# Two cross-attention layers on one core: another order of work inside a step

## The chip, the cores and the metric

The kernel runs on one core of one Trainium2 chip. The metric is the device time of one execution in microseconds (us), and for several executions their median. The core has five engines with a queue each: TensorE (PE in the profile; PEld is its weight load), VectorE (DVE), ScalarE (ACT), GpSimd (POOL) and SyncE (SP, which here only starts transfers). A queue is worked in order: an instruction that has to wait holds up all that stands behind it on its engine.

## The reference, cut to what matters

All numbers are float32. There are 8 batches of 256 rows with 320 channels (20 heads of 16), and for each batch 256 context tokens of 512 numbers. Two layers follow each other.

```python
# layer 0: 77 text tokens, 179 image tokens, two softmaxes, one sum
q, k, v = x @ Wq.T, enc[:, :77] @ Wk.T, enc[:, :77] @ Wv.T
k_ip, v_ip = enc[:, 77:] @ Wk_ip.T, enc[:, 77:] @ Wv_ip.T
out = softmax(q k.T / 4) v + softmax(q k_ip.T / 4) v_ip      # per head
x1 = out @ Wo.T + bo + x
# layer 1: 252 text tokens, 4 image tokens
q, k, v = x1 @ W_q, enc[:, :252] @ W_k, enc[:, :252] @ W_v
p = softmax(q k.T / 4)                                        # per head
sem = l2norm(p @ enc[:, :252]) . l2norm(enc[:, 252:])
p_ip = softmax(q k_ip.T / 4 + 0.5 * sem) * spatial_mask
out = (p v + p_ip v_ip) @ W_out + b_out + x1
```

The norm in `sem` comes from a Gram matrix: |p E|^2 = sum over t of p_t (p G)_t, with G = E E^T. So each head of layer 1 has one product that gives p G, p v and the dot products with the image tokens at once.

## The kernel before, in words

**Units and steps.** A unit is four heads ("a quad") of one batch and one layer; there are five units per batch and layer, 40 per layer. The loop at the end of the kernel runs over steps n = 5b + s. Step n handles unit n of layer 0 and unit n - 6 of layer 1, and the second half of the layer-1 unit of the step before. From n = 40 on there is only layer 1 (`layer_1`), before that `both_layers` writes out a step.

**Order.** TensorE, VectorE, ScalarE and GpSimd keep the order in which the program issues (`manual_schedule`); only the transfers that SyncE starts are placed by the framework's scheduler. So the order of the calls in `both_layers`, and the table `plan` in `fillers`, are the order of each of the four queues.

**What a step does.** For a layer-0 unit: `l0_begin` multiplies queries and keys (16 products, L317) into the four PSUM tiles sc0 to sc3; `l0_max` takes row maxima on VectorE (8 reductions, L412); `l0_exp` takes exponentials on ScalarE, one pair of heads per call (8 instructions, L424); `l0_transposed` turns one pair's probabilities on TensorE (8 transposes into the same sc tiles, L355) and copies them out (L360: three of four on VectorE, one on ScalarE); `l0_values` multiplies with v (L442, tile oT) and ScalarE copies the result; in the next step `l0_attn` turns it back (L462, tile o), scales it on VectorE (L467) and adds the text and image parts on GpSimd (L477).
For a layer-1 unit: `scores1` begins it and takes the maxima of both pairs (L612, with a small copy, L615); `l1_exp` (L624, 4 instructions per pair); `l1_transposed`; and in the next step `l1_values(v1, j)` for each head j and each half of the rows: two TensorE products (L648, L651) into a tile y, which VectorE reads with a multiply-and-sum (L655) and a small copy (L659).

**Fillers.** Work of other stages of a batch (projections of k, v and q, the Gram matrix, output projections, the rest of layer 1's image attention) is put between these by `fillers(n, place)`: step s and place give a list of functions for the batch ahead, now, last or old (b + 1, b, b - 1, b - 2). Nearly all of them write a tile "mm" on TensorE, which VectorE or ScalarE then copies out.

**PSUM.** sc0 to sc3 have one buffer each, the tiles "mm" two, and y, oT and o together two (tag "y"):

```python
ps_sc = ctx.enter_context(tc.tile_pool(name="ps_sc", bufs=1, space=PS))
ps_mm = ctx.enter_context(tc.tile_pool(name="ps_mm", bufs=2, space=PS))
ps_y = ctx.enter_context(tc.tile_pool(name="ps_y", bufs=2, space=PS))
```

So a tile "mm" can be written once the one two before it has been copied out, and the same holds for the tiles "y". The transposed attention and x tiles (`attn_T`, `transposed`) use "mm" too, one tile per half of the rows.

**Transfers.** `load_batch(b)` reads the transposed x and the transposed context of batch b, on SyncE (for batch 1 on ScalarE). It is called in step s = 3 of the batch before (s = 2 for batch 1). xT has one buffer, which it shares with the transposed x1; encT has two.

Of the kernel before, what the change touches and what calls it, by code (L numbers as in the profile page):

```python
# [8 lines left out]
F32 = mybir.dt.float32  # L9
# [41 lines left out]
def kernel(  # L51
# [67 lines left out]
    def load_batch(b, eng):  # L119
        r = {}  # L120
        r["xT"] = io.tile([P, NC, S], F32, tag="xT", name=f"xT_{b}", bufs=1)
        eng.dma_start(
            out=r["xT"][:, 0:2, :], in_=xT[b, 0:256, :].rearrange("(m p) s -> p m s", p=P)
        )
        eng.dma_start(out=r["xT"][:, 2, :], in_=xT[b, CH[2] :, :])
        r["encT"] = io.tile([P, NE, T], F32, tag="encT", name=f"encT_{b}")
        eng.dma_start(out=r["encT"], in_=encT[b].rearrange("(k p) t -> p k t", p=P))
        return r
# [9 lines left out]
    bat = {0: load_batch(0, nc.sync)}  # L138
# [345 lines left out]
    def l0_attn_T(b):  # L484
        r = bat[b]
        r["aT"] = [attn_T(r["attn"][:, half, :], f"p0_{b}_{half}") for half in range(NH)]

    def l0_out(b):
        r = bat[b]
        r["x1"] = bp.tile([P, NH, C], F32, tag="x1", name=f"x1_{b}")  # L490
        for half in range(NH):
            project_out(
                r["aT"][half], wo, r["x"][:, half, :], r["x1"][:, half, :], f"p0_{b}_{half}"
            )
# [248 lines left out]
    def l1_attn_T(b):  # L743
        r = bat[b]
        r["aT1"] = [attn_T(r["attn1"][half], f"p1_{b}_{half}") for half in range(NH)]

    def l1_out(b, half):
        r = bat[b]
        osb = work.tile([P, C], F32, tag="attn1", name=f"osb_{b}_{half}", bufs=3)
        project_out(r["aT1"][half], wo1, r["x1"][:, half, :], osb, f"p1_{b}_{half}")  # L750
        nc.sync.dma_start(out=out[b, half * P : (half + 1) * P, :], in_=osb)
# [24 lines left out]
    def fillers(n, place):  # L776
# [4 lines left out]
            (0, 1): [(l0_q, now, (2,)), (l0_attn_T, last)],  # L781
            (0, 2): [(l0_out, last)],
            (0, 3): [(l1_k, last, 0)],
            (0, 4): [(l1_xT, last)],
            (0, 5): [(l1_q, last, (0, 1))],
            (1, 0): [(l0_k, now, 1)],
            (1, 1): [(l1_k, last, 2)],
            (1, 3): [(l1_k, last, 1)],
            (1, 4): [(l1_gram, now, 0)],
            (2, 0): [(l1_v, now, 0)],  # L790
            (2, 1): [(l1_q, last, (2,)), (l1_norm, old)],
            (2, 3): [(l0_k, now, 2)],
            (2, 4): [(l1_fused, old)],
            (3, 0): [(l0_v, ahead, 0)],
            (3, 1): [(l1_v, now, 1), (l1_probs, old)],
            (3, 2): [(l1_probs_T, old)],
            (3, 3): [(l0_q, ahead, (0, 1))],
            (3, 4): [(l1_attn, old), (l1_image, now)],
            (4, 0): [(l0_k, ahead, 0)],
            (4, 1): [(l1_gram, now, 1), (l1_attn_T, old)],  # L800
            (4, 2): [(l1_out, old, 0)],
            (4, 3): [(l0_v, ahead, 1)],
            (4, 4): [(l1_out, old, 1)],
        }
        if n < NQ - 1:
# [6 lines left out]
                (1, 3): [(image_tokens, 0)],  # L812
# [5 lines left out]
                (3, 3): [(l0_q, 1, (0, 1)), (l1_image, 0)],  # L818
# [19 lines left out]
    def scores1(n):  # L838
# [4 lines left out]
        home = 1 if n < N0 else n % 2  # L843
        u = l1_begin(*divmod(n - SHIFT, NQ), home)
        for pair in range(2):
            l1_max(u, pair)
        return u

    def both_layers(n, u, v1):
# [6 lines left out]
        part(l0_attn, u)  # L856
        part(l1_values, v1, 0)
        l0_exp(u0, 1)
        part(l1_values, v1, 1)
        l0_transposed(u0, 0)  # L860
        fillers(n, 1)
        part(l1_values, v1, 2, (0,))
        l0_transposed(u0, 1)
        part(l1_values, v1, 2, (1,))
        qz[1] = queries(1, n)
        qz[0] = queries(0, n + 1)
        fillers(n, 2)
        u1 = scores1(n)
        part(l1_exp, u1, 0)
        fillers(n, 3)  # L870
        part(l1_exp, u1, 1)
        part(l1_values, v1, 3, (0,))
        part(l1_transposed, u1, 0)
        fillers(n, 4)
        part(l1_values, v1, 3, (1,))
        part(l1_transposed, u1, 1)
        fillers(n, 5)
# [4 lines left out]

# [91 lines left out]
```

## Time and profile before

| | us |
|---|---|
| median of 3 runs (lowest, highest) | 961.18 (959.59, 962.16) |
| the profiled execution: its own time | 962.78 |
| its span, first to last instruction | 961.1 |
| PE busy | 912.3 |
| DVE busy | 632.3 |
| ACT busy | 533.2 |
| POOL busy | 199.3 |

The mean granted TensorE clock was 0.986. Busy time of PE includes time in which a product waits for its weights, so it isn't all work. The timeline lists instructions by start; "xN" merges N instructions of one line, and a bracket gives the idle time of that engine just before and what ended it. Records of one engine overlap a little, so a duration in a stream is best read as the distance from one start to the next. In full batches the steps s = 0 to 4 take 26.04, 20.63, 20.27, 22.11 and 22.69 us, read from one oT (L442) to the next: 111.74 us a batch.

### The profile page before, as it was taken

How to read it: one execution, taken by the hardware profiler on the slowest of the kernel's cores; microseconds unless marked ns; L12 is line 12 of the kernel's file. 1: busy time of each engine (PE TensorE's matmuls, PEld its weight loads, DVE VectorE, ACT ScalarE, POOL GpSimd, SP SyncE). 2: the span in 40 equal slices, each digit the busy share in tenths (PEclk: the TensorE clock that was granted, in tenths of full speed). 3: DMA queues.
4: the chain of work that ended last, by engine and by line, in shares of the span. 5: the costliest groups of instructions: out<-in, count | busy, mean ns of one | idle time of the engine just before them, and what ended most of it. 6: DMA issues, size and time to landing. Idle time of an engine off the chain costs nothing.

```text
span 961.1 us, 18793 instructions
## 1 busy us (share of the span) xinstructions
PE 912.3 (95%) x6296; PEld 722.4 (75%) x6296; DVE 632.3 (66%) x2127; ACT 533.2 (55%) x2314; POOL 199.3 (21%) x336
## 2 busy tenths in 40 slices
PE   7888999999999999999999999999999999889885
PEld 5566678788787877778787887878777887667773
DVE  2344467766776677767776668766777677764864
ACT  3476466656554675546755566546655467433540
POOL 5421221222111221122211221112211222102100
PEclk9799999999999999999999999999999999999997
DMA  7310010001000010000100010000100000000000
GB/s 263 97 45 1 16 39 1 1 15 40 5 9 21 4 42 1 15 15 23 22 1 14 15 41 5 9 21 16 29 1 15 19 1 1 1 14 1 1 15 14
DMA packets 16847, 21.88 MB, mean 23 GB/s; under 512 B 1632, under 2 KB 15904, under 8 KB 16752
## 3 DMA queue, kind: packets, MB, share of 16 engines
q1 hardware_dynamic: 12048, 12.49, 4.9%
q0 software_dynamic: 1296, 4.25, 1.4%
q10 hardware_dynamic: 3408, 3.95, 1.2%
q8 instruction: 51, 0.84, 0.4%
q14 instruction: 44, 0.36, 0.1%
HBM read 17.24 MB, written 2.62 MB: 21 GB/s over the span
## 4 chain that ended last, share of the span: by engine, by line
PE 84%; ACT 8%; DVE 4%; issue 2%; DMA 1%; POOL 1%; ACTq 0%; DVEq 0%; POOLq 0%
PE y L648 15%; PE sc L355 13%; PE sc L317 9%; PE v L279 9%; PE y L651 7%; PE k L267 7%; PE q L249 6%; PE p_o L292 6%; PE oT L442 4%; ACT e L424 3%; ACT e L624 3%; PE g L525 2%; DVE nmx L612 2%; PE p_aT_ps L285 1%; DVE nmx L412 1%
## 5 line engine op out<-in xcount | busy, mean ns | idle before, releaser
L424 ACT ACTIVATE e<-sc,nmx 128x77 f32<-128x77 f32 (+1 forms) x640 | 227.6, 413 | 58.9 <-DVE nmx L412 58.9
L648 PE MATMUL y<-gv,et 126*128 126x272 f32 x640 | 210.3, 410 | 10.1 <-DVE num L659 6.0
L655 DVE CUSTOM_DVE_ANT_0 e<-y,e 128x252 f32<-128x252 f32 x320 | 134.3, 420 | 105.6 <-PE y L651 104.5
L624 ACT ACTIVATE e<-sc,nmx 128x252 f32<-128x252 f32 x320 | 147.2, 484 | 101.7 <-DVE aip L615 101.6
L355 PE MATMUL sc<-ident,e 128*126 128x128 f32 (+1 forms) x1280 | 173.5, 275 | 14.0 <-ACT e L424 7.8
L412 DVE TENSOR_REDUCE nmx<-sc 128x2 f32<-128x154 f32 x320 | 109.7, 416 | 97.2 <-PE sc L317 97.2
L360 DVE COPY et<-sc 128x512 f32<-128x512 f32 (+1 forms) x228 | 151.9, 688 | 23.3 <-PE sc L355 20.0
L355 PEld LDWEIGHTS sc<-ident,e 128*126 128x126 f32 (+1 forms) x1280 | 145.1, 140 | 26.2 <-ACT e L424 12.6
L424 ACT ACTIVATION_READ_ACCUMULATOR e<-sc,nmx 128x1 f32 x640 | 160.7, 251 | 0.0
L651 PEld LDWEIGHTS y<-gv,et 126*128 126x128 f32 x640 | 121.7, 190 | 26.2
L651 PE MATMUL y<-gv,et 126*128 126x146 f32 x640 | 132.0, 288 | 0.0
L648 PEld LDWEIGHTS y<-gv,et 126*128 126x128 f32 x640 | 102.3, 190 | 30.1 <-issue 11.1
L612 DVE TENSOR_REDUCE nmx<-sc 128x2 f32<-128x504 f32 x160 | 106.8, 676 | 26.6 <-PE sc L317 26.6
L360 ACT COPY et<-sc 128x512 f32<-128x512 f32 (+1 forms) x92 | 53.2, 585 | 96.4 <-PE sc L355 96.4
L317 PE MATMUL sc<-k,sc_qz 32*128 32x256 f32 x1280 | 99.3, 404 | 2.6 <-POOL sc_qz L306 2.5
L477 POOL TENSOR_TENSOR attn<-o_sb 128x64 f32<-128x64 f32 x80 | 24.0, 321 | 364.0 <-DVE o_sb L467 358.1
L317 PEld LDWEIGHTS sc<-k,sc_qz 32*128 32x128 f32 x1280 | 62.6, 185 | 33.6 <-issue 23.2
L306 POOL TENSOR_SCALAR sc_qz<-q,quad_m 128x256 f32<-128x256 f32 x80 | 73.1, 925 | 4.2 <-ACT q L256 4.2
L267 PE MATMUL k<-encT,wk 128*128 128x77 f32 (+1 forms) x384 | 72.7, 332 | 0.0
L624 ACT ACTIVATION_READ_ACCUMULATOR e<-sc,nmx 128x1 f32 x320 | 70.1, 219 | 0.0
L267 PEld LDWEIGHTS k<-encT,wk 128*128 128x128 f32 x384 | 57.9, 190 | 15.4 <-issue 12.0
L538 POOL COPY gv<-gv 126x3402 f32<-126x3402 f32 (+1 forms) x16 | 33.2, 2078 | 121.4 <-PE sc L355 71.5
(129 smaller groups left out, 1059.1 us busy)
## 6 DMA issues: line engine op xcount, KB each, us to landing
encT<-in_encT_dram SPq DMA_DIRECT2D x7, 512.0 KB
x<-in_x_dram SPq DMA_DIRECT2D x8, 320.0 KB
out_dram<-osb SPq DMA_DIRECT2D x16, 160.0 KB
xT<-in_xT_dram SPq DMA_DIRECT2D x7, 256.0 KB
xT<-in_xT_dram SPq DMA_DIRECT2D x7, 128.0 KB
vip_rows<-vipA SPq DMA_DIRECT2D x32, 25.0 KB
wk<-in_WkT_dram ACTq DMA_DIRECT2D x1, 640.0 KB
wkip<-in_WkipT_dram ACTq DMA_DIRECT2D x1, 640.0 KB
```

Source lines behind the costliest of these rows:

```text
L267: nc.tensor.matmul(ps[:, t0:t1], columns(w, k, m), encT_b[:, k, t0:t1], start=(k == 0), stop=(k == NE - 1),)
L279: nc.tensor.matmul(ps, lhsT(k), w[:, k, :], start=(k == 0), stop=(k == NE - 1))
L317: nc.tensor.matmul(sc[j][:, half, :], qz[rows, half * P : (half + 1) * P], kT(j)[rows, m, :], start=True, stop=True,)
L355: nc.tensor.transpose(v[:, c, half, :], u["e"][x][:, j, half, t0 + c * tn : t0 + (c + 1) * tn], ident,)
L360: copies[j](u["et"][x][:tn, j].rearrange("p c n s -> p (c n s)"), ps)
L412: nc.vector.tensor_reduce(u["nmx"][x][:, j, :, a], u["sc"][2 * x + j][:, :, t0:t1], AX.X, ALU.max, negate=True,)
L424: nc.scalar.activation(u["e"][x][:, j, half, t0:t1], u["sc"][2 * x + j][:, half, t0:t1], AF.Exp, bias=u["nmx"][x][:, j, half, a : a + 1], ...
L612: nc.vector.tensor_reduce(u["nmx"][x][:, j, :], sc[:, :, t0 : t0 + TXT1], AX.X, ALU.max, negate=True)
L624: nc.scalar.activation(u["e"][x][:, j, half, t0 : t0 + TXT1], u["sc"][2 * x + j][:, half, t0 : t0 + TXT1], AF.Exp, bias=u["nmx"][x][:, j, ...
L648: nc.tensor.matmul(y, et[:, 1 - odd, half, :], gv[0][:, g, full], start=True, stop=False)
L651: nc.tensor.matmul(y[:, into], et[:, odd, half, :], gv[1][:, g, part], start=False, stop=True)
L655: nc.vector.tensor_tensor_reduce(e, y[:, g0 : g0 + TXT1], e, op0=ALU.mult, op1=ALU.add, scale=1.0, scalar=0.0, accum_out=r["n2"][:, half, ...
```

## The change

- `both_layers` is written in another order. `l0_attn` moves from ahead of the first layer-1 products to behind them and a filler; the first two heads' products, which stood in a row, are now parted by a filler, `l0_attn` and the first transposes; the third head's two halves, which stood on either side of the second transposes, now both follow them. There are seven filler places in place of six.
- `scores1` is split into `begin1` and `max_exp1`, which takes the maxima and the exponentials of one pair. In `both_layers` no filler stands between the two pairs' exponentials any more. In `layer_1` two filler places come ahead of the scores, and the second pair's maxima move behind the first head's products.
- `l0_attn_T`, `l1_attn_T` and `l0_out` take one half of the rows per call, and the table puts the halves at different places.
- The table of fillers is rewritten: the Gram matrix' second part goes from step 4 to step 3, the next batch's first v from step 3 to step 2, and the places are renumbered; the table for the first four steps likewise.
- `load_batch` is split; the context of batch b + 1 is loaded in step s = 2.

```diff
@@ -116,16 +116,16 @@
     def load_e(t, w, eng):
         eng.dma_start(out=t[:, :, 0:C], in_=w.rearrange("(k p) c -> p k c", p=P))
 
-    def load_batch(b, eng):
-        r = {}
-        r["xT"] = io.tile([P, NC, S], F32, tag="xT", name=f"xT_{b}", bufs=1)
-        eng.dma_start(
-            out=r["xT"][:, 0:2, :], in_=xT[b, 0:256, :].rearrange("(m p) s -> p m s", p=P)
-        )
-        eng.dma_start(out=r["xT"][:, 2, :], in_=xT[b, CH[2] :, :])
-        r["encT"] = io.tile([P, NE, T], F32, tag="encT", name=f"encT_{b}")
-        eng.dma_start(out=r["encT"], in_=encT[b].rearrange("(k p) t -> p k t", p=P))
-        return r
+    def load_xT(b, eng):
+        t = io.tile([P, NC, S], F32, tag="xT", name=f"xT_{b}", bufs=1)
+        eng.dma_start(out=t[:, 0:2, :], in_=xT[b, 0:256, :].rearrange("(m p) s -> p m s", p=P))
+        eng.dma_start(out=t[:, 2, :], in_=xT[b, CH[2] :, :])
+        bat[b]["xT"] = t
+
+    def load_encT(b, eng):
+        t = io.tile([P, NE, T], F32, tag="encT", name=f"encT_{b}")
+        eng.dma_start(out=t, in_=encT[b].rearrange("(k p) t -> p k t", p=P))
+        bat[b]["encT"] = t
 
     def load_resid(b):
 
@@ -135,7 +135,9 @@
         for half in range(NH):
             nc.gpsimd.tensor_tensor(r["x"][:, half, :], r["x"][:, half, :], bo_b, ALU.add)
 
-    bat = {0: load_batch(0, nc.sync)}
+    bat = [{} for _ in range(B)]
+    load_xT(0, nc.sync)
+    load_encT(0, nc.sync)
     wq, wq1 = new_c("wq", HP), new_c("wq1", HP)
     wo, wo1 = new_c("wo"), new_c("wo1")
     wk, wkip, wk1 = new_e("wk", again=HP), new_e("wkip", again=HP), new_e("wk1", again=HP)
@@ -481,17 +483,17 @@
                 ALU.add,
             )
 
-    def l0_attn_T(b):
-        r = bat[b]
-        r["aT"] = [attn_T(r["attn"][:, half, :], f"p0_{b}_{half}") for half in range(NH)]
-
-    def l0_out(b):
-        r = bat[b]
-        r["x1"] = bp.tile([P, NH, C], F32, tag="x1", name=f"x1_{b}")
-        for half in range(NH):
-            project_out(
-                r["aT"][half], wo, r["x"][:, half, :], r["x1"][:, half, :], f"p0_{b}_{half}"
-            )
+    def l0_attn_T(b, half):
+        r = bat[b]
+        r["aT", half] = attn_T(r["attn"][:, half, :], f"p0_{b}_{half}")
+
+    def l0_out(b, half):
+        r = bat[b]
+        if half == 0:
+            r["x1"] = bp.tile([P, NH, C], F32, tag="x1", name=f"x1_{b}")
+        project_out(
+            r["aT", half], wo, r["x"][:, half, :], r["x1"][:, half, :], f"p0_{b}_{half}"
+        )
 
 
     def l1_k(b, m):
@@ -740,14 +742,14 @@
             attn = r["attn1"][half]
             nc.vector.tensor_tensor(attn, attn, ps[:, :C], ALU.add)
 
-    def l1_attn_T(b):
-        r = bat[b]
-        r["aT1"] = [attn_T(r["attn1"][half], f"p1_{b}_{half}") for half in range(NH)]
+    def l1_attn_T(b, half):
+        r = bat[b]
+        r["aT1", half] = attn_T(r["attn1"][half], f"p1_{b}_{half}")
 
     def l1_out(b, half):
         r = bat[b]
         osb = work.tile([P, C], F32, tag="attn1", name=f"osb_{b}_{half}", bufs=3)
-        project_out(r["aT1"][half], wo1, r["x1"][:, half, :], osb, f"p1_{b}_{half}")
+        project_out(r["aT1", half], wo1, r["x1"][:, half, :], osb, f"p1_{b}_{half}")
         nc.sync.dma_start(out=out[b, half * P : (half + 1) * P, :], in_=osb)
 
     msk = const.tile([P, NH], F32, tag="msk", name="msk")
@@ -778,29 +780,31 @@
         ahead, now, last, old = b + 1, b, b - 1, b - 2
         plan = {
             (0, 0): [(l0_v, now, 2)],
-            (0, 1): [(l0_q, now, (2,)), (l0_attn_T, last)],
-            (0, 2): [(l0_out, last)],
-            (0, 3): [(l1_k, last, 0)],
-            (0, 4): [(l1_xT, last)],
-            (0, 5): [(l1_q, last, (0, 1))],
+            (0, 1): [(l0_q, now, (2,))],
+            (0, 2): [(l0_attn_T, last, 0)],
+            (0, 3): [(l0_attn_T, last, 1), (l0_out, last, 0), (l0_out, last, 1)],
+            (0, 4): [(l1_k, last, 0)],
+            (0, 5): [(l1_xT, last)],
+            (0, 6): [(l1_q, last, (0, 1))],
             (1, 0): [(l0_k, now, 1)],
             (1, 1): [(l1_k, last, 2)],
-            (1, 3): [(l1_k, last, 1)],
-            (1, 4): [(l1_gram, now, 0)],
+            (1, 4): [(l1_k, last, 1)],
+            (1, 5): [(l1_gram, now, 0)],
             (2, 0): [(l1_v, now, 0)],
             (2, 1): [(l1_q, last, (2,)), (l1_norm, old)],
-            (2, 3): [(l0_k, now, 2)],
-            (2, 4): [(l1_fused, old)],
-            (3, 0): [(l0_v, ahead, 0)],
-            (3, 1): [(l1_v, now, 1), (l1_probs, old)],
-            (3, 2): [(l1_probs_T, old)],
-            (3, 3): [(l0_q, ahead, (0, 1))],
-            (3, 4): [(l1_attn, old), (l1_image, now)],
+            (2, 4): [(l0_k, now, 2)],
+            (2, 5): [(l0_v, ahead, 0), (l1_fused, old)],
+            (3, 0): [(l1_v, now, 1)],
+            (3, 1): [(l1_gram, now, 1), (l1_probs, old)],
+            (3, 3): [(l1_probs_T, old)],
+            (3, 4): [(l0_q, ahead, (0, 1))],
+            (3, 5): [(l1_attn, old), (l1_image, now)],
             (4, 0): [(l0_k, ahead, 0)],
-            (4, 1): [(l1_gram, now, 1), (l1_attn_T, old)],
-            (4, 2): [(l1_out, old, 0)],
-            (4, 3): [(l0_v, ahead, 1)],
-            (4, 4): [(l1_out, old, 1)],
+            (4, 1): [(l1_attn_T, old, 0)],
+            (4, 2): [(l1_attn_T, old, 1)],
+            (4, 3): [(l1_out, old, 0)],
+            (4, 4): [(l0_v, ahead, 1)],
+            (4, 5): [(l1_out, old, 1)],
         }
         if n < NQ - 1:
             plan = {
@@ -809,13 +813,13 @@
                 (0, 2): [(l0_v, 0, 2)],
                 (1, 0): [(l0_k, 0, 1)],
                 (1, 1): [(l0_q, 0, (2,))],
-                (1, 3): [(image_tokens, 0)],
+                (1, 4): [(image_tokens, 0)],
                 (2, 0): [(l1_gram, 0, 0)],
                 (2, 1): [(l1_v, 0, 0)],
                 (2, 2): [(l0_k, 0, 2)],
                 (3, 0): [(l1_v, 0, 1)],
                 (3, 1): [(l0_v, 1, 0)],
-                (3, 3): [(l0_q, 1, (0, 1)), (l1_image, 0)],
+                (3, 4): [(l0_q, 1, (0, 1)), (l1_gram, 0, 1), (l1_image, 0)],
             }
         for f, at, *args in plan.get((s, place), ()):
             if 0 <= at < B:
@@ -835,16 +839,16 @@
         if u is not None:
             f(u, *args)
 
-    def scores1(n):
+    def begin1(n):
 
         if qz[1] is None:
             return None
 
-        home = 1 if n < N0 else n % 2
-        u = l1_begin(*divmod(n - SHIFT, NQ), home)
-        for pair in range(2):
-            l1_max(u, pair)
-        return u
+        return l1_begin(*divmod(n - SHIFT, NQ), 1 if n < N0 else n % 2)
+
+    def max_exp1(u, x):
+        l1_max(u, x)
+        l1_exp(u, x)
 
     def both_layers(n, u, v1):
 
@@ -853,49 +857,50 @@
             l0_max(u0, pair)
         l0_exp(u0, 0)
         fillers(n, 0)
-        part(l0_attn, u)
         part(l1_values, v1, 0)
         l0_exp(u0, 1)
+        fillers(n, 1)
+        part(l0_attn, u)
+        l0_transposed(u0, 0)
         part(l1_values, v1, 1)
-        l0_transposed(u0, 0)
-        fillers(n, 1)
-        part(l1_values, v1, 2, (0,))
+        fillers(n, 2)
         l0_transposed(u0, 1)
-        part(l1_values, v1, 2, (1,))
+        part(l1_values, v1, 2)
         qz[1] = queries(1, n)
         qz[0] = queries(0, n + 1)
-        fillers(n, 2)
-        u1 = scores1(n)
-        part(l1_exp, u1, 0)
         fillers(n, 3)
-        part(l1_exp, u1, 1)
+        u1 = begin1(n)
+        part(max_exp1, u1, 0)
+        part(max_exp1, u1, 1)
+        fillers(n, 4)
         part(l1_values, v1, 3, (0,))
         part(l1_transposed, u1, 0)
-        fillers(n, 4)
+        fillers(n, 5)
         part(l1_values, v1, 3, (1,))
         part(l1_transposed, u1, 1)
-        fillers(n, 5)
+        fillers(n, 6)
         l0_values(u0)
         return u0, u1
 
     def layer_1(n, u, v1):
 
+        fillers(n, 0)
+        fillers(n, 1)
         part(l0_attn, u)
-        u1 = scores1(n)
-        part(l1_exp, u1, 0)
-        fillers(n, 0)
+        u1 = begin1(n)
+        part(max_exp1, u1, 0)
         part(l1_values, v1, 0)
-        fillers(n, 1)
-        part(l1_exp, u1, 1)
+        fillers(n, 2)
+        part(max_exp1, u1, 1)
         part(l1_values, v1, 1)
-        fillers(n, 2)
+        fillers(n, 3)
+        fillers(n, 4)
         part(l1_values, v1, 2)
-        fillers(n, 3)
         part(l1_transposed, u1, 0, COPIES[1][1:] * 2)
-        fillers(n, 4)
+        fillers(n, 5)
         part(l1_transposed, u1, 1)
         part(l1_values, v1, 3)
-        fillers(n, 5)
+        fillers(n, 6)
         return None, u1
 
     l0_q(0, (0, 1))
@@ -906,8 +911,10 @@
         b, s = divmod(n, NQ)
         if s == 1 and 0 < b < B:
             load_resid(b)
+        if s == 2 and b + 1 < B:
+            load_encT(b + 1, nc.sync if b else nc.scalar)
         if s == (3 if b else 2) and b + 1 < B:
-            bat[b + 1] = load_batch(b + 1, nc.sync if b else nc.scalar)
+            load_xT(b + 1, nc.sync if b else nc.scalar)
         before = (both_layers if n < N0 else layer_1)(n, *before)
         if n + 1 >= N0:
             qz[1] = queries(1, n + 1)
```

## The prediction

> **What bounds the kernel now.** I read the page first: parts 1 and 4, then part 5.
>
> ```profile
> span 961.1 us, 18793 instructions
> PE 912.3 (95%) x6296; PEld 722.4 (75%) x6296; DVE 632.3 (66%) x2127; ACT 533.2 (55%) x2314; POOL 199.3 (21%) x336
> PE 84%; ACT 8%; DVE 4%; issue 2%; DMA 1%; POOL 1%; ACTq 0%; DVEq 0%; POOLq 0%
> ```
>
> TensorE carries the chain, so only what shortens or lengthens its queue counts. Its 95% hides waits, since a product held at its weights still counts as busy. So next I read TensorE's timeline of a step s = 1 (n = 26), and VectorE's beside it:
>
> ```profile
> 546.80 0.62 PE L648 MATMUL y<-gv,et 126*128 126x272 f32 x2
> 547.26 0.41 PE L651 MATMUL y<-gv,et 126*128 126x146 f32 x2
> 547.59 0.73 PE L648 MATMUL y<-gv,et 126*128 126x272 f32 x2
> 548.15 0.41 PE L651 MATMUL y<-gv,et 126*128 126x146 f32 x2
> 548.39 0.67 PE L648 MATMUL y<-gv,et 126*128 126x272 f32 x2
> ...
> 550.04 1.04 PE L355 MATMUL sc<-ident,e 128*128 128x128 f32 x8
> ```
>
> ```profile
> 548.60 0.42 DVE L655 CUSTOM_DVE_ANT_0 e<-y,e 128x252 f32<-128x252 f32 x1 [0.37 <-PE y L651]
> 548.94 0.17 DVE L659 COPY num<-y 128x20 f32<-128x20 f32 x1
> ```
>
> A product pair needs 0.71 us start to start where nothing holds it (0.46 + 0.25). Four in a row (546.80 to 550.04) take 3.24, 0.40 too much: each waits for VectorE to free one of two tiles. From o to the first transposes it is 3.41 to 3.47 us in nearly every step 7 to 37, against 0.22 + 4 x 0.71 = 3.06.
>
> The third view is the end of step s = 2, and the two steps in which the fillers run out:
>
> ```profile
> 470.86 0.66 PE L355 MATMUL sc<-ident,e 128*126 128x128 f32 x4 [0.25 <-ACT e L624]
> 471.45 1.07 PE L442 MATMUL oT<-et,v 128*32 128x256 f32 x16
> 472.45 1.73 PE L317 MATMUL sc<-k,sc_qz 32*128 32x256 f32 x16
> ```
>
> ```profile
> 834.30 0.72 PE L648 MATMUL y<-gv,et 126*128 126x272 f32 x2 [2.07 <-DVE o_sb L467]
> 873.92 1.15 PE L317 MATMUL sc<-k,sc_qz 32*128 32x256 f32 x16 [1.77 <-POOL sc_qz L306]
> ```
>
> Scores take 1.08; the 1.73 at 472.45 waits for copies that VectorE makes behind `l1_fused`.
>
> **What the Trainium skill says.** "TensorE: Matmul & The Clock Gate" (architectural detail of the array): ScalarE and VectorE are strict FIFO; TensorE may pull weight loads ahead. The trace agrees: a k copy below stands exactly where the program put it. "PSUM — Partial Sum Buffer" (PSUM: the matmul accumulator): 8 banks of 2 KiB. Tiles sc, mm and y fill 4 + 2 + 2, so no ring can grow. "ScalarE: Activation LUTs" (What ACT_TABLE_LOAD costs): about 1283 ns for the load; the page of this trace shows 1283.
>
> **The sum without waits.** From start-to-start medians: scores 1.08, eight transposes 0.87 (layer 1: 0.89), oT 1.0, o 0.22, k of layer 0 2.21, of layer 1 1.8 (1.7 in s = 1's first place), v 2.26, q 1.30 or 2.70, Gram 1.70 and 0.88, a transposed half 0.33, an output half 1.62, probs_T 0.32, image attention 1.08. Steps s = 0 to 4 come to 25.15, 19.99, 18.37, 21.12 and 21.82, together 106.45. Measured are 26.04, 20.63, 20.27, 22.11 and 22.69, 111.74. So 5.3 us a batch are waits, the most that a new order can win; no product is added or removed.
>
> **Part by part, full steps (n = 7 to 37).** I place the new order by these durations, t from the end of the layer-0 scores.
>
> *Heads apart, `l0_attn` later.* The maxima end at 2.7, y00 and y01 run at about 2.3 to 3.7 into two free tiles, VectorE has read them by 4.3; o comes at 4.0 (s = 4, shortest filler) to 5.5 and needs only y00. The next pair comes after the transposes, when o is read. The waits of the row go: 0.36 to 0.41 a step. The third head now stands between the second transposes and layer 1's scores, so ScalarE's copy of sc3 is done: that wins the 0.16 (s = 1) and about 0.47 (s = 2, behind the table load for the square root) that these scores lose. The halved `attn_T` wins about 0.2 in s = 0: its second half no longer waits for q's copy.
>
> *A v in s = 2 instead of s = 3.* It comes before the second layer-1 transposes: their wait (0.35) and the 0.6 at 472.45 go. The context it needs is issued by SyncE at 446.41 already, ahead of its place in the program; I give the earlier load nothing. If it were late, v would wait, but it has over 20 us. Batch 1's three loads stay in step 2 on ScalarE's queue (issued at 48.0 to 49.4 before, 1.2 us of issuing), only the context first: nothing won or lost. `l1_image` keeps its place behind the first layer-1 transposes; SyncE issues its four row copies early (462.3) and GpSimd's part (0.73) has over 10 us before its reader, so it costs nothing either.
>
> *No filler between the exponentials.* Here I find a new wait. ScalarE in s = 1:
>
> ```profile
> 557.02 0.47 ACT L624 ACTIVATE e<-sc,nmx 128x252 f32<-128x252 f32 x1 [1.97 <-DVE aip L615]
> ...
> 558.82 0.38 ACT L499 COPY k<-k 128x252 f32<-128x252 f32 x1
> 559.07 0.30 ACT L500 COPY k<-k 128x126 f32<-128x126 f32 x1
> 559.23 0.52 ACT L624 ACTIVATE e<-sc,nmx 128x252 f32<-128x252 f32 x1
> ```
>
> The k copies now fall behind all eight exponentials: 0.87 + 8 x 0.45 + 0.1 + 0.4 = 5.0 us after the scores, not 3.1. In s = 0 the second tile of x1's transposes takes the buffer of that k, as the start shows:
>
> ```profile
> 101.27 0.55 PE L285 MATMUL x1T_ps<-ident,x 128*128 128x128 f32 x3 [0.30 <-ACT k L500]
> ```
>
> It comes at 1.8 + 0.71 + 0.89 + 0.33 = 3.7 and waits 1.3; behind it stand the third head's last product, transposes, q and oT. In s = 3 the second image-attention product (at 4.8) likewise waits for q's copy (5.15): 0.35. In the other steps the tile two before is long copied.
>
> *Gram's second part in s = 3.* GpSimd's gv copy (1.13) now stands ahead of the additions (0.6) and the masked queries (0.92). It starts when ScalarE has done both exponential halves and the Gram copy, 7.2; so queries are ready at 9.95, scores are due at 9.7: 0.3 lost.
>
> Waits left: s = 0 1.3, s = 2 0.6 (first layer-1 transposes behind the second table load, as now), s = 3 0.65, and 0.1 a step for what I don't see: 3.05. A batch takes 109.5, 2.25 less; 31 steps are 6.2 batches: **14.0 us**.
>
> **Steps 38 and 39.** No v or k is left for place 0, so VectorE's maxima lie open (2.07 and 1.69 us idle). Step 38 now has v and the Gram part there, step 39 transposes. By the same placing they take 19.0 and 19.7, against 22.31 and 22.26: **5.9**.
>
> **Start (n below 7).** Exponentials bound these steps: what TensorE does before the second transposes is covered, what comes after is not. Two fillers move under this cover: a v of 2.15 in n = 0, of which 0.9 remains as gain (the second exponentials end only a little later), and a k of 2.1 in n = 2. The Gram part moves out of cover in n = 3: -0.9. Small ones 0.7. **2.8**.
>
> **Tail (from 851).** A k of 1.7 stands ahead of step 41's scores and covers the 1.77 on GpSimd. In the others VectorE's order changes: second maxima behind the first head. Placed likewise, steps 40, 44, 45 win 0.6, 1.0, 0.5, steps 42 and 43 nothing (l1_norm, l1_probs now delay the scores): **4.0**, with 2 either way.
>
> Sum 14.0 + 5.9 + 2.8 + 4.0 = 26.7. From the span of 961.1 this leaves 934.4. The profiled execution's own time (962.78) is 1.7 over its span and 1.6 over the median (961.18), so the median's forecast is 961.2 - 26.7 = 934.5; I say **935**.
>
> **Rivals.** *Copies late in more places (948).* My placing has ends only 0.1 to 0.5 apart in s = 3 and 4. If ScalarE's late copies or GpSimd's queue cost 0.4 us more in each of 33 steps, 13 of the 27 are gone. For it: ten places use the two "mm" tiles in s = 0. Against it: only two have a copy on ScalarE less than two tiles before.
> *Slower: transposes too early (over 964, say 972).* Second transposes of layer 0 move from 9.0 to 6.8 (s = 3, 4) to 8.4 after the scores; the exponentials end at 6.65 (551.0 in n = 26), 6.95 behind a v copy. The slack is 0 to 1.5, on average 0.7. Were the exponentials later by d, TensorE would lose d - 0.7 a step: from d = 1.5 on the gain is spent, at d = 1.8 it is 972. Against it: ahead of them ScalarE's order is unchanged and the maxima start as before.
> *Nothing (961).* VectorE sets the pace in the rows and the waits move to the next tile. Against it: VectorE is idle over 1 us between the groups.
> *More (923).* The start has TensorE at half clock around 36 to 50 (8 products of L279 4.42 us, not 2.15). If less idling spares that, about 6 us more, and step 0's new wait may be shorter.
>
> **Chances.** Forecast 0.61, late copies 0.16, more 0.10, nothing 0.04, slower 0.09. My forecast's own range is 927 to 942; with the late copies up to 953 and a little of "more", 926 to 953. The changes beyond 0.3% (about what a measurement of this kernel tells from none): faster 0.87, within 0.04, slower 0.09.
>
> **What would show it.** Right: from scores to transposes no y with more than 0.46 + 0.25; the 1.73 gone; a wait of about 1.3 at x1's second transpose for ACT's k copy (L500), six times; step 41's scores without the 1.77. Wrong: waits of L355 for ACT e in many steps, or scores for GpSimd outside s = 3. The forecast breaks most easily at ScalarE's order, which I placed by hand.

## The result and the profile after

| | before | after |
|---|---|---|
| median (lowest, highest), us | 961.11 (959.59, 962.16) | 944.51 (944.09, 945.82) |
| ratio of the times, 95% interval | | 0.983 (0.981 to 0.985) |
| the profiled execution: its own time | 962.78 | 944.11 |
| its span | 961.1 | 942.4 |

The change makes the kernel 1.7% faster. Medians fell by 16.6 us, the two profiled spans by 18.7; the forecast was 26.7 off the span and a time of 935, in a range of 926 to 953. The page of the changed kernel, parts 1 and 4:

```profile
span 942.4 us, 18840 instructions
PE 893.2 (95%) x6296; PEld 715.4 (76%) x6296; DVE 626.4 (66%) x2127; ACT 530.8 (56%) x2314; POOL 199.3 (21%) x336
PE 66%; issue 15%; ACT 9%; DVE 5%; POOL 3%; DMA 1%; ACTq 0%; POOLq 0%; DVEq 0%
```

TensorE's busy share is 95% as before, while 19 us of its busy time are gone. Most of it lies at products that stood held at their tiles: 8.7 us at the first product of a pair (L648, 210.3 before, 201.6 now), 5.2 us at the scores (99.3 and 94.1). The chain seems to have left TensorE (84% before, 66% now, with 15% "issue"), but this is how it was traced back: in each step s = 3 it follows a short wait on GpSimd (below) into that engine's queue, where 20.6 us of idleness lie ahead; six such pieces, 122.7 us together, are most of the "issue". The bound is TensorE's queue still.

New line numbers are two higher (L648 is now L650). TensorE's timeline of a step s = 1 (n = 26), where the prediction showed four products in a row:

```profile
541.43 0.62 PE L650 MATMUL y<-gv,et 126*128 126x272 f32 x2
541.89 0.41 PE L653 MATMUL y<-gv,et 126*128 126x146 f32 x2
542.14 0.62 PE L650 MATMUL y<-gv,et 126*128 126x272 f32 x2
542.60 0.41 PE L653 MATMUL y<-gv,et 126*128 126x146 f32 x2
542.85 1.86 PE L269 MATMUL k<-encT,wk 128*128 128x252 f32 x8
544.55 0.38 PE L464 MATMUL o<-ident,oT_sb 128*128 128x128 f32 x2
544.77 1.04 PE L357 MATMUL sc<-ident,e 128*128 128x128 f32 x8
```

Every pair takes 0.46 + 0.25 us from start to start, and o takes 0.22, as where nothing holds it. The 1.73 at the end of s = 2 is gone as well: those scores start at 579.86 and take 1.07. What came instead is in the table of TensorE's waits (total us, times, longest):

```profile
PE x1T_ps L287 <- ACT k L502: 7.8, 7, 1.3
PE sc L357 <- ACT e L426: 7.3, 11, 1.0
...
PE sc L357 <- ACT e L626: 5.3, 16, 1.0
...
PE sc L319 <- POOL sc_qz L308: 2.6, 7, 0.6
...
PE ipo L735 <- ACT q L258: 1.1, 5, 0.2
```

The first is the forecast's new wait: 1.25 us in each of six steps s = 0 (n = 10 to 35), and the 0.30 that n = 5 had before. TensorE and ScalarE around it in n = 25:

```profile
529.86 1.06 PE L357 MATMUL sc<-ident,e 128*126 128x128 f32 x8
530.75 0.49 PE L287 MATMUL x1T_ps<-ident,x 128*128 128x128 f32 x3
532.49 0.55 PE L287 MATMUL x1T_ps<-ident,x 128*128 128x128 f32 x3 [1.25 <-ACT k L502]
```

```profile
528.28 0.47 ACT L626 ACTIVATE e<-sc,nmx 128x252 f32<-128x252 f32 x1 [6.24 <-DVE aip L617]
...
531.42 0.50 ACT L626 ACTIVATE e<-sc,nmx 128x252 f32<-128x252 f32 x1
531.87 0.41 ACT L501 COPY k<-k 128x252 f32<-128x252 f32 x1
532.12 0.32 ACT L502 COPY k<-k 128x126 f32<-128x126 f32 x1
```

TensorE has x1's first half transposed at 531.2 and has nothing to do until ScalarE has worked off the eight exponentials and the k behind them. ScalarE itself had been idle 6.24 us before the row. No instruction here is slow; the wait comes from the order.

Where the 18.7 us of the profiles come from, read from one oT to the next:

| part | forecast gain | gain |
|---|---|---|
| start, up to the oT of n = 6 | 2.8 | 0.8 |
| steps 7 to 37 | 14.0 | 8.4 |
| steps 38, 39 | 5.9 | 4.5 |
| tail | 4.0 | 5.1 |

Two rows of this table hold chance. Up to the oT of n = 6 the six profiled executions with the old start took 120.3 to 122.4 us, of which the one above is the longest; the four with the start of the change took 121.6 to 124.6. So the 0.8 isn't a gain that repeats. In steps 38 and 39, 1.4 of the 4.5 are a stretch of half clock in the profiled execution of before (experiment 8). The medians, 16.6 us apart, don't rest on one execution.

And a full batch, with the waits against the prediction's sum without waits (a v of 2.18 moved from s = 3 into s = 2, the Gram part of 0.88 from s = 4 into s = 3):

| step | before | after | without waits, new order | waits forecast | waits found |
|---|---|---|---|---|---|
| s = 0 | 26.04 | 26.71 | 25.15 | 1.4 | 1.56 |
| s = 1 | 20.63 | 20.16 | 19.99 | 0.1 | 0.17 |
| s = 2 | 20.27 | 21.56 | 20.55 | 0.7 | 1.01 |
| s = 3 | 22.11 | 20.80 | 19.82 | 0.75 | 0.98 |
| s = 4 | 22.69 | 21.08 | 20.94 | 0.1 | 0.14 |
| batch | 111.74 | 110.31 | 106.45 | 3.05 | 3.86 |

### The profile page after: what moved, and what is told of

Its sections match the earlier page's. It is cut to its first block, busy times and chain, and to the rows that moved or that the text cites. A ratio compares the mean times of both kernels' runs of the same rounds, so it can differ in the third digit from the quotient of the medians.

```text
span 942.4 us, 18840 instructions
## 1 busy us (share of the span) xinstructions
PE 893.2 (95%) x6296; PEld 715.4 (76%) x6296; DVE 626.4 (66%) x2127; ACT 530.8 (56%) x2314; POOL 199.3 (21%) x336
## 4 chain that ended last, share of the span: by engine, by line
PE 66%; issue 15%; ACT 9%; DVE 5%; POOL 3%; DMA 1%; ACTq 0%; POOLq 0%; DVEq 0%
PE y L650 11%; PE sc L357 10%; PE sc L319 8%; PE v L281 6%; PE k L269 6%; PE p_o L294 6%; PE y L653 6%; PE q L251 5%; ACT e L626 5%; PE oT L444 4%; ACT e L426 4%; DVE nmx L614 2%; POOL sc_qz L308 2%; PE g L527 2%; PE p_aT_ps L287 1%
## 5 line engine op out<-in xcount | busy, mean ns | idle before, releaser
L626 ACT ACTIVATE e<-sc,nmx 128x252 f32<-128x252 f32 x320 | 145.8, 479 | 124.3 <-DVE aip L617 120.7
L650 PE MATMUL y<-gv,et 126*128 126x272 f32 x640 | 201.6, 396 | 3.8 <-DVE num L661 3.7
L357 PE MATMUL sc<-ident,e 128*126 128x128 f32 (+1 forms) x1280 | 171.3, 275 | 12.8 <-ACT e L426 7.3
L650 PEld LDWEIGHTS y<-gv,et 126*128 126x128 f32 x640 | 104.4, 190 | 18.0 <-issue 4.7
L319 PE MATMUL sc<-k,sc_qz 32*128 32x256 f32 x1280 | 94.1, 404 | 2.9 <-POOL sc_qz L308 2.6
L319 PEld LDWEIGHTS sc<-k,sc_qz 32*128 32x128 f32 x1280 | 58.9, 185 | 32.5 <-issue 21.7
L269 PE MATMUL k<-encT,wk 128*128 128x77 f32 (+1 forms) x384 | 72.8, 332 | 0.7 <-DMA wk<-in_WkT_dram 0.7
L269 PEld LDWEIGHTS k<-encT,wk 128*128 128x128 f32 x384 | 58.1, 190 | 16.3 <-issue 12.6
L626 ACT ACTIVATION_READ_ACCUMULATOR e<-sc,nmx 128x1 f32 x320 | 68.4, 214 | 0.0
```

Source lines behind the costliest of these rows:

```text
L269: nc.tensor.matmul(ps[:, t0:t1], columns(w, k, m), encT_b[:, k, t0:t1], start=(k == 0), stop=(k == NE - 1),)
L319: nc.tensor.matmul(sc[j][:, half, :], qz[rows, half * P : (half + 1) * P], kT(j)[rows, m, :], start=True, stop=True,)
L357: nc.tensor.transpose(v[:, c, half, :], u["e"][x][:, j, half, t0 + c * tn : t0 + (c + 1) * tn], ident,)
L626: nc.scalar.activation(u["e"][x][:, j, half, t0 : t0 + TXT1], u["sc"][2 * x + j][:, half, t0 : t0 + TXT1], AF.Exp, bias=u["nmx"][x][:, j, ...
L650: nc.tensor.matmul(y, et[:, 1 - odd, half, :], gv[0][:, g, full], start=True, stop=False)
```

## The experiments

Times are medians, with the ratio to the kernel before and its 95% interval; the kernel before had medians of 960.0 to 960.5 beside them. Steps are compared in the profiled executions, where a step of a full batch repeats from batch to batch within 0.02 us, but for a few that are 0.1 to 0.3 us longer.

**1. The exponentials apart again.** On the changed kernel: the filler back between the two pairs' exponentials, nothing else.

```diff
         u1 = begin1(n)
-        part(max_exp1, u1, 0)
-        part(max_exp1, u1, 1)
+        part(l1_max, u1, 0)
+        part(l1_max, u1, 1)
+        part(l1_exp, u1, 0)
         fillers(n, 4)
+        part(l1_exp, u1, 1)
```

> The changed kernel with one thing undone: in a step with both layers a filler stands again between the exponentials of the two layer-1 pairs (the order of before). Theory (ScalarE's copies come too late): x1's second transpose waits 1.25 us seven times for ACT's k copy (7.8 us in the table of waits, 1.4 to 1.5 us with the restart) and the second image product 0.5 us five times for q's copy; both waits go, 944.5 - 7 x 1.45 - 5 x 0.5 = 932 us, and steps s = 0 fall from 26.71 to 25.3. Rival (the transposes behind the exponentials become the wait once a copy stands between the exponentials): the second layer-1 transposes wait instead, and the time stays at 942 to 945 us.

Measured: 934.58, ratio 0.973 (0.970 to 0.976); 9.9 us below the changed kernel. s = 0 takes 25.24 in place of 26.71, s = 3 20.30 in place of 20.80. ScalarE's timeline of this kernel in the same step, n = 25:

```profile
525.04 0.48 ACT L626 ACTIVATE e<-sc,nmx 128x252 f32<-128x252 f32 x1
525.48 0.38 ACT L501 COPY k<-k 128x252 f32<-128x252 f32 x1
525.73 0.30 ACT L502 COPY k<-k 128x126 f32<-128x126 f32 x1
525.89 0.52 ACT L626 ACTIVATE e<-sc,nmx 128x252 f32<-128x252 f32 x1
```

The k stands between the pairs again, and all of x1's transposes run through without a wait. The rival was that exponentials pulled apart would delay the second layer-1 transposes by as much; TensorE's waits for ScalarE's layer-1 exponentials are 5.5 us in all, against 5.3.

**2. The exponentials together, alone.** The opposite, on the kernel before: the filler behind both pairs.

```diff
         part(l1_exp, u1, 0)
-        fillers(n, 3)
         part(l1_exp, u1, 1)
+        fillers(n, 3)
```

> The kernel before with one part of the change alone: the filler between the two pairs' layer-1 exponentials moves behind both. Theory: x1's second transpose waits for the k copy in the six or seven steps s = 0, 1.2 to 1.4 us each, the second image product 0.3 to 0.5 us five times, and a little is won at the second layer-1 transposes of s = 2: 961.1 + 9 = 970 us. Rival (no cost, TensorE has slack there): 961 us.

Measured: 971.58, 1.012 (1.009 to 1.016). s = 0 loses 1.46, s = 3 0.77, s = 2 wins 0.27. The table of TensorE's waits has just the two entries that the changed kernel brought:

```profile
PE x1T_ps L285 <- ACT k L500: 7.8, 7, 1.3
...
PE ipo L733 <- ACT q L256: 1.1, 5, 0.2
```

So this one part costs 10 to 11.5 us, whether it is taken out of the new order or put into the old one. It is the largest loss that was found inside the change.

**3. The heads apart, alone.** On the kernel before, the second head's products behind the first transposes; `l0_attn` stays ahead.

```diff
-        part(l1_values, v1, 1)
         l0_transposed(u0, 0)
+        part(l1_values, v1, 1)
         fillers(n, 1)
```

> The kernel before with one part of the change alone: the second head's products stand behind the first transposes, so no more than two product pairs are in a row; all else is as before. Theory (VectorE's pace in the row costs 0.36 to 0.41 us a step): 31 full steps lose that wait, and steps 38 and 39 gain little, 961.1 - 12 = 949 us; no pair above 0.72 us between layer-0 scores and transposes. Rival (the waits only move): with the first transposes 1.8 us earlier TensorE waits for the exponentials or for VectorE's copies, and the time is 957 to 961 us.

Measured: 953.96, 0.994 (0.992 to 0.996). Each full step wins 0.23 us, not the 0.38 that were looked for. TensorE's timeline shows the rest still there:

```profile
429.57 0.38 PE L462 MATMUL o<-ident,oT_sb 128*128 128x128 f32 x2
429.79 0.62 PE L648 MATMUL y<-gv,et 126*128 126x272 f32 x2
430.25 0.41 PE L651 MATMUL y<-gv,et 126*128 126x146 f32 x2
430.58 0.73 PE L648 MATMUL y<-gv,et 126*128 126x272 f32 x2
431.14 0.41 PE L651 MATMUL y<-gv,et 126*128 126x146 f32 x2
```

With o ahead, three tiles of the tag "y" are still asked for in a row: the two pairs take 0.79 and 0.81, not 0.71.

**4. The heads apart, and o behind the first head.** As the change does, but with no filler between that head and o.

```diff
-        part(l0_attn, u)
         part(l1_values, v1, 0)
         l0_exp(u0, 1)
-        part(l1_values, v1, 1)
+        part(l0_attn, u)
         l0_transposed(u0, 0)
+        part(l1_values, v1, 1)
         fillers(n, 1)
```

> The kernel before with the heads apart and l0_attn moved: two product pairs, then l0_attn, the first transposes, then the other two pairs; the fillers stay where they were. The run with the heads apart alone won 0.23 us a step and left 0.15 us between the first and the second pair. Theory (those 0.15 us are the wait for the tile that o holds until VectorE has read it behind the maxima): they go too, the step wins 0.38, 961.1 - 12 = 949 us. Rival (o, now behind two pairs with no filler between, waits for the first pair's tile, because VectorE is in the maxima until 2.7 us after the scores): what is won at the pairs is lost at o, and the time stays near 954 us.

Measured: 953.57, 0.992 (0.991 to 0.994), no more than experiment 3. Now the pairs are free and o has the wait:

```profile
432.03 0.62 PE L648 MATMUL y<-gv,et 126*128 126x272 f32 x2
432.49 0.41 PE L651 MATMUL y<-gv,et 126*128 126x146 f32 x2
432.90 0.41 PE L462 MATMUL o<-ident,oT_sb 128*128 128x128 f32 x2
```

0.41 from the pair's second product to o, where 0.25 are needed: the rival held. The wait moves to whichever tile comes third. In the changed kernel, where nothing is held, a filler stands between (L269 in the timeline of after) and gives VectorE the time. The two single moves won 0.17 to 0.24 a step; the full 0.38 came only with the row's whole order.

**5. v and the Gram part back to their steps.** On the changed kernel, for all but the first batch's Gram part.

```diff
-            (2, 5): [(l0_v, ahead, 0), (l1_fused, old)],
-            (3, 0): [(l1_v, now, 1)],
-            (3, 1): [(l1_gram, now, 1), (l1_probs, old)],
+            (2, 5): [(l1_fused, old)],
+            (3, 0): [(l0_v, ahead, 0)],
+            (3, 1): [(l1_v, now, 1), (l1_probs, old)],
...
-            (4, 1): [(l1_attn_T, old, 0)],
+            (4, 1): [(l1_gram, now if n >= NQ else B, 1), (l1_attn_T, old, 0)],
```

> The changed kernel with the places of before for three fillers: the next batch's first v in step 3, place 0; layer 1's second v in step 3, place 1; the Gram matrix' second part in step 4, place 1 (batch 0's stays where the change put it). Theory: the wait of the second layer-1 transposes in s = 2 and the scores' wait of 0.6 us behind it return (5 to 6 times 0.95), the scores' wait for GpSimd in s = 3 goes (6 times 0.36), and step 38 loses its cover at place 0 (2 to 3 us): 944.5 + 5.5 = 950 us. Rival (these moves were even, the gain came from elsewhere): 943 to 946 us.

Measured: 946.88, 0.986 (0.984 to 0.988): 2.4 us above the changed kernel, between the theory and the rival, and the two intervals overlap. The profiles say more. Steps s = 2 to 4 take 64.08 together, in place of 63.44: the last scores of s = 2 take 1.94 from start to start (471.04 to 472.98) in place of 1.07, and the wait for GpSimd in s = 3 goes. So the moves are worth 0.64 us in a full batch, 2.4 us over the steps 7 to 37. The expected loss in steps 38 and 39 didn't come. Step 38 took 19.0, less than the 19.94 of after: the Gram part's 0.88 has left it, and in step 39 this part falls into o's wait for VectorE, which shrinks from 1.39 to 0.52, and costs nothing there.

One more difference in this execution isn't the edit's: n = 6, whose order is the same in both kernels, took 20.16 in place of 17.19, at a granted clock of 0.51 from 115 to 122 us (1.00 in after). Its own time, 948.3, is 3 us above the lower two of the four runs.

**6. GpSimd's Gram copy behind the queries.** On the changed kernel, the copy of gv becomes a function of its own and is called two places later.

```diff
...
-            (3, 3): [(l1_probs_T, old)],
+            (3, 3): [(l1_spread, now, 1), (l1_probs_T, old)],
...
```

> The changed kernel with one queue's order altered: GpSimd's spreading of the Gram matrix' second part is issued in place 3 of step 3, behind the masked queries, not in place 1 ahead of them. Theory (GpSimd's copy of 1.13 us makes the scores of s = 3 wait 0.29 us, 0.36 with the restart): these waits go in six steps, 944.5 - 2.2 = 942.3 us, and TensorE waits for GpSimd's queries only at the start and in the tail. Rival (VectorE's or ScalarE's copy of sc is due at the same time): another wait takes its place, 944.5 us.

Measured: 941.14, 0.980 (0.979 to 0.981); 3.4 us below the changed kernel. s = 3 falls from 20.80 to 20.43, and its wait for GpSimd is gone. In steps 7 to 37 this makes 2.6 us; the rest isn't explained by it. In the changed kernel, the timeline of GpSimd and TensorE in s = 3:

```profile
588.40 1.13 POOL L540 COPY gv<-gv 126x1134 f32<-126x1134 f32 x1 [20.62 <-ACT gv L536]
589.50 0.60 POOL L479 TENSOR_TENSOR attn<-o_sb 128x64 f32<-128x64 f32 x2
590.07 1.83 POOL L308 TENSOR_SCALAR sc_qz<-q,quad_m 128x256 f32<-128x256 f32 x2
591.05 1.15 PE L319 MATMUL sc<-k,sc_qz 32*128 32x256 f32 x16 [0.29 <-POOL sc_qz L308]
```

The copy has no reader in this step, yet the masked queries, for which the scores wait, stand behind it on GpSimd's queue. This is the 0.3 of the forecast, in the place that it named.

**7. The first batch's Gram part back in n = 4.** On the changed kernel, it goes from step 3's table to step 4's.

```diff
-            (4, 1): [(l1_attn_T, old, 0)],
+            (4, 1): [(l1_gram, 0 if n < NQ else B, 1), (l1_attn_T, old, 0)],
...
-                (3, 4): [(l0_q, 1, (0, 1)), (l1_gram, 0, 1), (l1_image, 0)],
+                (3, 4): [(l0_q, 1, (0, 1)), (l1_image, 0)],
```

> The changed kernel with batch 0's second Gram part back in step 4, between the exponentials' waits, and no longer in step 3 behind them. Theory (the start lost what it should have won because that part left its cover, and because step 4's TensorE then idled long enough to fall to half clock: its v took 3.36 us, not 2.24): steps 3 and 4 get back to 12.6 and 11.8 us from 14.2 and 13.3, 944.5 - 3 = 941.5 us. Rival (half clock at the start is chance): only the 0.9 us of the part itself, 943.6 us.

Measured: 942.09, 0.981 (0.979 to 0.982); 2.4 us below the changed kernel. n = 3 takes 13.31 in place of 14.20, n = 4 11.80 in place of 13.34. The first is the 0.9 of the prediction. The second wasn't foreseen. TensorE in n = 4, changed kernel:

```profile
79.13 0.66 PE L357 MATMUL sc<-ident,e 128*128 128x128 f32 x4 [1.02 <-ACT e L426]
80.53 1.11 PE L357 MATMUL sc<-ident,e 128*128 128x128 f32 x4 [0.74 <-ACT e L426]
81.44 3.43 PE L281 MATMUL v<-wvip,encT 128*128 128x320 f32 x8
84.80 1.07 PE L444 MATMUL oT<-et,v 128*32 128x256 f32 x16
```

The v takes 3.36 from start to start; with the Gram part back it takes 2.25. The table by stretches shows the clock under it (window, its length, busy time of PE, PEld, DVE, ACT and POOL, then the granted clock, DMA share and GB/s). The changed kernel, and then experiment 7:

```profile
75.00:80.00 5.00, 3.02 (x20) 2.13 (x19) 3.19 (x9) 5.00 (x30) 1.50 (x3) 1.00 0.00 0
80.00:85.00 5.00, 4.47 (x16) 3.05 (x20) 0.76 (x2) 1.15 (x5) 0.00 (x0) 0.66 0.00 0
```

```profile
75.00:80.00 5.00, 3.85 (x29) 3.14 (x27) 3.27 (x9) 5.00 (x31) 0.00 (x0) 1.00 0.00 0
80.00:85.00 5.00, 4.39 (x40) 2.88 (x44) 0.84 (x2) 2.21 (x8) 2.59 (x4) 1.00 0.01 3
```

The Gram part's 0.88 made the difference between 60% and 77% busy, and behind the 60% came a stretch of half clock. The changed kernel and experiments 1, 5 and 6, which have the Gram part in n = 3, all have a dip of the clock between 80 and 88, and n = 4 takes 13.3 to 13.5 in them. The nine other kernels profiled here, which have it in n = 4, have no dip there and take 11.8.

**8. The tail alone.** On the kernel before, from n = 40 on the order and the table of the change (some 40 lines; the core is the new `layer_1` of the diff above).

> The kernel before with the changed order of the last ten steps alone (those with layer 1 only: two filler places ahead of the scores, the second pair's maxima behind the first head's products, halved transposes). Theory: the queries' wait of 1.77 us at step 41 is covered by a k, and small gains in steps 44 and 45: 961.1 - 5 = 956 us. Rival (the gain of the end comes from steps 38 and 39 and the tail's order is even): 960 to 961 us.

Measured: 955.33, 0.995 (0.994 to 0.997): 4.7 us. From the oT of n = 39 to the end its profile has 104.0 us, the kernel before 109.8, the changed one 104.8. GpSimd's waits of L317 fall from 2.5 to 0.7 us.

This profile also clears up something else. It doesn't touch step 38, and yet that takes 20.87 in it and 22.31 in the profile of before. The stretches, of the kernel before:

```profile
806.00:812.00 6.00, 4.40 (x42) 2.67 (x42) 5.24 (x18) 3.20 (x16) 0.00 (x0) 1.00 0.00 0
812.00:816.00 4.00, 3.80 (x12) 3.18 (x13) 1.61 (x10) 3.65 (x22) 3.77 (x6) 0.57 0.00 0
```

Experiment 8:

```profile
812.00:816.00 4.00, 4.00 (x23) 3.41 (x24) 2.75 (x14) 3.39 (x20) 3.77 (x6) 1.00 0.02 4
```

Both have the same wait of 1.7 us ahead, but the profiled execution of before had a stretch of half clock behind it, and 1.44 us of its step 38 are that. The execution of experiment 9 below, with the same step 38, has it too: 22.31 us, at a clock of 0.57 from 810 to 814.

**9. The context loaded a step sooner, alone.** On the kernel before, `encT` of the next batch at s = 2.

```diff
...
+        if s == 2 and b + 1 < B:
+            ctx_next = load_encT(b + 1, nc.sync if b else nc.scalar)
         if s == (3 if b else 2) and b + 1 < B:
             bat[b + 1] = load_batch(b + 1, nc.sync if b else nc.scalar)
+            bat[b + 1]["encT"] = ctx_next
```

> The kernel before with one part of the change alone: the next batch's context is asked for in step 2, not in step 3. Theory (SyncE issued it early already, and its first reader stays where it was): no change, 960 to 961 us. Rival (the earlier place in the program moves other transfers or a wait on SyncE): 958 or less, or 963 or more.

Measured: 960.85, 1.000 (0.999 to 1.001). SyncE starts that transfer at 444.4 in place of 446.4. By these 2 us the whole execution is ahead since its start, so the transfer has not moved: it had gone out early already.

**10. Better than both.** The edits of experiments 1, 6 and 7 together on the changed kernel:

> The changed kernel with three edits together: the filler back between layer 1's exponentials, the Gram spreading behind the queries in step 3, and batch 0's second Gram part back in step 4. Theory: the three add up, 934.6 - 2.2 - 3 = 929.4 us. Rival (with the first wait gone, the next is due within a few tenths): 932 to 934 us.

Measured: 927.61, 0.966 (0.965 to 0.967). s = 0 and s = 3 take 25.24 and 19.95, a batch 107.97. And then, in step 2, the v and `l1_fused` also ahead of the first layer-1 transposes:

```diff
-            (2, 4): [(l0_k, now, 2)],
-            (2, 5): [(l0_v, ahead, 0), (l1_fused, old)],
+            (2, 4): [(l0_k, now, 2), (l0_v, ahead, 0), (l1_fused, old)],
```

> The version with three edits (filler back between the exponentials, Gram spreading behind the queries, batch 0's Gram part back), and in step 2 the next batch's v and l1_fused at place 4, ahead of the first layer-1 transposes, not at place 5 behind them. Theory (these transposes come 0.85 us too early, since the exponentials stand behind the second table load): they wait no more, 927.6 - 5 x 0.8 = 923.5 us. Rival (v's copy and the exponential of l1_fused now stand between the two pairs' exponentials, so the second transposes wait instead): 926 to 930 us.

Measured: 923.98, 0.963 (0.960 to 0.965), some 2% under the changed kernel. s = 2 falls from 21.55 to 20.80. The waits of TensorE for layer 1's exponentials, first of the three edits, then of all four (L631 is the changed kernel's L626):

```profile
PE sc L357 <- ACT e L631: 5.5, 17, 1.0
```

```profile
PE sc L357 <- ACT e L631: 3.6, 8, 1.0
```

The transposes of s = 2 had waited 0.83 a batch for exponentials behind the table load; with the v ahead of them they no longer do.

## Why the prediction was right, and where its sizes were off

The sign and the range held; 944.5 is 9.5 above the time forecast and outside the likeliest case's own range of 927 to 942. The mechanisms that it named were found; the gain came out smaller because waits were left out or put too low.

*Heads apart, `l0_attn` later: right.* No pair is held in the row. Layer 1's scores in s = 2, which now follow the third head, take 1.07 in place of 1.39, also with the v back in s = 3 (experiment 5). And s = 1 and s = 4, which have no other new wait, are 0.17 and 0.14 from the sum without waits. Experiments 3 and 4 add what the prediction only assumed: the moves don't add up one by one, since the wait went to o or to a pair until a filler parted them.

*No filler between the exponentials: right in place and size.* 1.25 against 1.3, six times; 0.39 against 0.35 for the image product in s = 3. Both directions of the edit confirm it (experiments 1 and 2). "Late copies in more places", the rival at 948, comes near the time but not by its mechanism: beside these two only one other tile in the table of waits of the whole trace waits for a copy on ScalarE, 0.5 us.

*A v in s = 2, Gram in s = 3: right, one term too small.* The scores' 1.73 became 1.07, and experiment 5 loses this again. "0.6" for the first layer-1 transposes of s = 2 was 0.37 + 0.46 = 0.83, since each half of the transposes waits on its own exponentials; with their restart s = 2 has 1.01 where 0.7 were put. s = 3 has 0.98 where 0.75 were put: 0.29 for GpSimd as forecast, the image product's 0.39 and another 0.10 behind it, 0.08 at a head, and some 0.1 not traced. Together with s = 0 the mis-sized term, "waits left 3.05", measured 3.86: 0.81 a batch, 5.0 of the 5.6 us that steps 7 to 37 fell short. The rest lies in the steps of the first and the last batch, which have other fillers than the five that I added up.

*Steps 38 and 39: the baseline was wrong.* 5.9 came from 22.31 and 22.26 down to 19.0 and 19.7. The steps take 19.94 and 20.18, and in both the first layer-1 transposes wait 1.03 + 0.25 for exponentials, which the prediction's text doesn't have. In step 39, o waits 1.39 for VectorE besides; the prediction doesn't say whether its 19.7 held that. And 1.44 of the 22.31 was a stretch of half clock, which two of three executions have and one hasn't (experiment 8). Against the 20.87 without it the change wins 3.0 here, not 4.5; the prediction read a step's time from one record and took all of it for waits.

*Start: n = 4 had no term.* The "-0.9 in n = 3" was right: experiment 7 gets back 0.89 there. (n = 3 lost 1.65, but the other 0.76 only lies at its border: the oT that opens it takes 1.78 from start to start in place of 1.00, held for ScalarE's copy, and n = 2 ends sooner by that.) But n = 4 lost 1.54, and experiment 7 gets back just this. I had asked what work moves out of cover, but not what the idling left behind does to the clock. "TensorE: Matmul & The Clock Gate" of the Trainium skill (Part 1: The HAM clock gate) puts the fall to half clock behind a window of about 3.4 us of idleness; here no wait ahead of it was longer than 1.02 us, TensorE idled 2 us in 5, and ahead of the half clock of step 38 in before the longest wait was 1.69 us. The measurement decides: half clock came without so long a gap.

*Tail: a little too low,* 5.1 against 4.0, within the 2 given; experiment 8, with the tail alone, has 5.8.

*The context: right,* nothing (experiment 9). *Transposes too early,* the slower rival, isn't seen: waits of layer 0's transposes for exponentials are 7.3 us, against 7.8, and between 120 and 800 us there is none. *Nothing* is refuted by the result, and *more* by the start: most of its half clock around 36 to 50 stayed. The 1283 ns of the table load, which the prediction reads from the page, stand in the trace's view by lines.

Two things stay open. That idling sets the clock of n = 4 rests on the kernels in which it happens, four with and nine without, not on a run that changes the idling and nothing else. The Gram part's products also break up a stretch, 75.7 to 81.4 us in after, in which TensorE does nothing but transposes; a rival is that these count for less than other products, and no run parts the two. And why the same steps 6 and 38 get a stretch of half clock in one execution and none in another wasn't followed.

## What to carry to other kernels

When work is moved, list for each queue what now stands behind what: the filler that was taken from between two rows of exponentials carried a copy with it (of k in s = 0, of q in s = 3), and the place of these copies, not the filler's own products, cost 10 us. Tiles in a small ring must be counted in the order in which all their users come, since parting two of them can just hand the wait to the third. And before a step's time is taken as a baseline, look at its granted clock and at the same step in another batch.

## What was not expected of the hardware

A product that is held at its tile can cost more than the wait: in the old row the pair behind the wait took 0.56 from first to second product, not 0.46 (547.59 to 548.15 before). Its weights start to load at 547.58, 0.01 us ahead of it; those of the free pair (546.80) do so 0.11 us ahead. The same 0.56 stands where a pair follows scores directly and no tile holds it (811.30 to 811.86 after, weights from 811.30), so it goes with the late load, not with the hold alone.

Stretches of half clock come behind as little as 1.7 us of idleness (806 to 816 above), and the same idleness passes without one in another execution, as do the 2.07 us of step 39 (834.30 before). The two that the tables show lasted 3.4 us each: the clock granted inside them is 0.50 (81 to 83 us in after, 813 to 815 in before), and the shares missing from the windows, 0.34 of 5 us and 0.43 of 4 us, are half of 3.4 us both times.
